# High and low halves on alternating rows of a head, moved straight from the staged tile; the second batch's norm at the start

## The chip, the cores and the metric

The kernel runs on one core of one Trainium2 chip. The core has TensorE (PE, with its weight loads shown as PEld), VectorE (DVE), ScalarE (ACT), GpSimd (POOL) and SyncE (SP), each with its own instruction stream that is carried out in order, a memory SBUF of 128 partitions, here also called rows, in which tiles live, and PSUM banks that the matmuls write. DMA transfers are issued by SP, ACT or POOL and carried out by 16 DMA engines. The metric is the time of one execution on the device in microseconds.

## The reference

Two layers, each of self-attention, cross-attention over a context, and a gated feed-forward, all with a norm before and a residual after. Four batches of 512 rows with 320 features, 20 heads of 16, a context of 1601 rows of 192. Everything is float32.

```python
def _attn(x, ctx, wq, wk, wv, wo, bo, heads):
    ...
    q = (x @ wq).reshape(b, n, heads, dh).transpose(0, 2, 1, 3)
    k = (ctx @ wk).reshape(b, j, heads, dh).transpose(0, 2, 1, 3)
    v = (ctx @ wv).reshape(b, j, heads, dh).transpose(0, 2, 1, 3)
    sim = jnp.einsum('bhid,bhjd->bhij', q, k) * scale
    a = jax.nn.softmax(sim, axis=-1)
    out = jnp.einsum('bhij,bhjd->bhid', a, v)
    out = out.transpose(0, 2, 1, 3).reshape(b, n, heads * dh)
    return out @ wo + bo
h1 = _ln(x, n1_g, n1_b)
x = _attn(h1, h1, q1, k1, v1, o1_w, o1_b, heads) + x
h2 = _ln(x, n2_g, n2_b)
x = _attn(h2, context, q2, k2, v2, o2_w, o2_b, heads) + x
h3 = _ln(x, n3_g, n3_b)
proj = h3 @ ff_w1 + ff_b1
a, g = jnp.split(proj, 2, axis=-1)
ff = a * jax.nn.gelu(g, approximate=False) @ ff_w2 + ff_b2
```

## The kernel before

**Units.** The work is cut into units: a layer, a kind (self, cross, ff), a batch and, for attention, a group of 4 heads. A layer has 20 self units (4 batches x 5 groups), then 20 cross units, then 4 feed-forward units. An attention unit goes over its keys in chunks of 128: a self unit has 4 chunks, a cross unit 13. In a chunk, `main` computes transposed scores for each of 4 heads (`st`, L1190), ScalarE takes the exponential (`pr`, L1200), and TensorE multiplies with the values (`av`, L1214); GpSimd adds the results of the chunks (L1231).

**The maximum of each row** is needed before the exponentials. It is found one or two units ahead: scores the other way round (`sps`, L990), the maximum by VectorE (L1007), at the end of which `max_end` turns the 16 columns of maxima, and four small transfers of 4 KB spread them into the rows of `nrows` (L1070). A third matmul of each score, over `nrows` and a tile of ones, subtracts the maximum. TensorE cannot start a unit's scores to their end before `nrows` has landed.

**High and low halves.** A float32 number is split into a high part (float32r) and the low rest, by GpSimd's `split` (L684, L685) into two staged tiles, `high` and `low`, whose rows are (head, feature): 64 rows for a group. In the tiles that the matmuls read, `kT` and `q`, a head has 32 rows, 16 high and then 16 low; `q` holds two such variants, high over low and low over high, so that two matmuls over 32 rows sum all four products. Since 16 rows of a head do not follow on each other in the same way in the staged tile and in `kT`, the halves go by way of memory: `move` first writes them to `kway` and `qway` (`on_way`), in a shape with heads outermost, and later reads them back into `kT` and `q` (`read_queries`, `reads`). Unit 0 alone does it with 24 transfers of 16 rows (L798), spread over the queues of SP, ACT and POOL.

**Order of the work.** The program is written out by a planner in Python. Tasks lie in chains, each with a cost and a due time in rounds; a chunk has two rounds. `steps` takes the most urgent task that is ready and for which there is credit. `both` is the projection of queries and keys of a self unit (L765), `queries` (L820) and `keys_of_context` (L849) those of a cross unit. Moves are not tasks: each unit holds a queue of them (`u.moves`), and `carry`, called at the end of `steps`, so once a chunk, emits them in the order of units, when enough rounds have passed since the unit's last one and while its `room` of 3 lasts; after them it emits `errands`, among which are the row maxima of cross units, if any room is left. All of these are issued by SP (L729 for the moves). A unit's maxima may begin four rounds after its last move was emitted (`at_hand`). `way_free` keeps a third unit from being projected while two are on the way; `free` and `unread` keep reads out of buffers whose former reader has scores left to emit.

**The start** is written by hand at the end of the function: batch 0 is loaded and normed, unit 0 projected, moved at once, its maxima found between projections for unit 1, and so on. `load_x(1)` is issued after the maxima of unit 0; the second batch's norm runs later as tasks.

**The output** of a batch goes to memory (`oway`, L1105) and comes back as `aT` with rows (head, feature) (L1114), beside `wo` in the same row order, for the output projection (L1124).

## Time and profile before

| | us |
|---|---|
| median of 3 runs | 3357.38 (3355.6 to 3358.45) |
| the profiled execution | 3351.58 |
| its span, first to last instruction | 3349.8 |

The profile is of one execution; its time is the one beside it in the table, and durations from it are compared with that one. Shares of busy time are means over stages of quite different kind. Some lines of the page beside those that are shown with the argument:

```profile
DVE  4667877776776777622237878776766767775221
ACT  2556667676676676821126765677767767776110
...
DMA packets 208849, 243.49 MB, mean 73 GB/s; under 512 B 60440, under 2 KB 140452, under 8 KB 208484
## 3 DMA queue, kind: packets, MB, share of 16 engines
q1 hardware_dynamic: 207900, 237.76, 22.7%
...
HBM read 129.25 MB, written 106.89 MB: 70 GB/s over the span
```

The two rows of digits are the busy tenths of VectorE and ScalarE in 40 equal slices of the span: the two low places, in the middle and at the end, are the feed-forward stages. The queue q1 is that of SP and carries nearly all that is moved.

### The profile page before, as it was taken

How to read it: one execution, taken by the hardware profiler on the slowest of the kernel's cores; microseconds unless marked ns; L12 is line 12 of the kernel's file. 1: busy time of each engine (PE TensorE's matmuls, PEld its weight loads, DVE VectorE, ACT ScalarE, POOL GpSimd, SP SyncE). 2: the span in 40 equal slices, each digit the busy share in tenths (PEclk: the TensorE clock that was granted, in tenths of full speed). 3: DMA queues.
4: the chain of work that ended last, by engine and by line, in shares of the span. 5: the costliest groups of instructions: out<-in, count | busy, mean ns of one | idle time of the engine just before them, and what ended most of it. 6: DMA issues, size and time to landing. Idle time of an engine off the chain costs nothing.

```text
span 3349.8 us, 81113 instructions
## 1 busy us (share of the span) xinstructions
PE 3113.5 (93%) x34290; PEld 1642.0 (49%) x34290; DVE 2105.4 (63%) x2841; ACT 1965.0 (59%) x3909; POOL 1131.7 (34%) x1230
## 2 busy tenths in 40 slices
PE   7889999899898899999999999998989989999999
PEld 4445445455444445445554554544544544543555
DVE  4667877776776777622237878776766767775221
ACT  2556667676676676821126765677767767776110
POOL 2334233434433433400213432344344344333000
PEclk7899999899998999999999999999998999999999
DMA  3344223212212222110014332322212212212000
GB/s 92 109 135 142 92 91 91 88 59 69 89 63 66 79 75 62 57 40 0 28 52 129 126 121 76 103 67 70 75 54 76 76 53 76 75 42 74 9 10 15
DMA packets 208849, 243.49 MB, mean 73 GB/s; under 512 B 60440, under 2 KB 140452, under 8 KB 208484
## 3 DMA queue, kind: packets, MB, share of 16 engines
q1 hardware_dynamic: 207900, 237.76, 22.7%
q8 instruction: 269, 4.41, 0.5%
q14 instruction: 96, 0.79, 0.1%
q0 software_dynamic: 288, 0.27, 0.0%
q10 hardware_dynamic: 296, 0.27, 0.0%
HBM read 129.25 MB, written 106.89 MB: 70 GB/s over the span
## 4 chain that ended last, share of the span: by engine, by line
PE 69%; DMA 11%; DVE 9%; ACT 5%; SPq 4%; issue 2%; POOL 1%; ACTq 0%; POOLq 0%; DVEq 0%
PE st L1190 20%; PE av L1214 16%; PE fps L1320 8%; PE yps L1374 5%; DVE pm L1007 4%; DMA nrows<-turned 4%; ACT pr L1200 3%; DMA q<-qway 3%; PE sps L990 3%; PE vps L932 3%; PE kps L849 3%; PE ops L1124 2%; PE qkps L765 2%; PE fps L1333 2%; SPq L1070 2%
## 5 line engine op out<-in xcount | busy, mean ns | idle before, releaser
L1200 ACT ACTIVATE pr<-st 128x512 f32<-128x512 f32 (+1 forms) x2720 | 1405.2, 603 | 511.6 <-PE st L1190 447.8
L1007 DVE TENSOR_REDUCE pm<-sps 128x2 f32<-128x1024 f32 (+1 forms) x987 | 1134.7, 1188 | 288.6 <-PE sps L990 175.5
L1231 POOL TENSOR_TENSOR o<-o,vo 128x512 f32<-128x512 f32 x576 | 739.7, 1284 | 1442.5 <-ACT vo L1230 1406.4
L1190 PE MATMUL st<-q,kT 32*128 32x512 f32 (+1 forms) x5120 | 980.2, 452 | 23.5 <-DVE pm L1007 7.2
L990 PE MATMUL sps<-kT,q 32*128 32x512 f32 x4800 | 874.2, 454 | 67.2 <-DMA q<-qway 37.9
L1214 PE MATMUL av<-pr,vals 128*32 128x512 f32 (+1 forms) x5440 | 774.6, 638 | 37.9 <-ACT pr L1200 31.9
L1190 PEld LDWEIGHTS st<-q,kT 32*128 32x128 f32 (+1 forms) x5120 | 478.9, 187 | 527.9 <-ACT pr L1200 301.9
L1190 PE MATMUL st<-nrows,ones 32*128 32x512 f32 (+1 forms) x2720 | 645.9, 414 | 92.8 <-DMA nrows<-turned 92.6
L1007 DVE TENSOR_REDUCE nmax<-sps 128x2 f32<-128x1024 f32 (+1 forms) x349 | 380.1, 1129 | 178.1 <-PE sps L990 146.9
L990 PEld LDWEIGHTS sps<-kT,q 32*128 32x128 f32 x4800 | 389.6, 193 | 122.6 <-DVE pm L1007 33.4
L1190 PEld LDWEIGHTS st<-nrows,ones 32*128 32x128 f32 (+1 forms) x2720 | 334.0, 189 | 138.6 <-DMA nrows<-turned 103.9
L1230 ACT COPY vo<-av 128x512 f32<-128x512 f32 x576 | 347.8, 604 | 71.9 <-PE av L1214 65.8
L1320 PE MATMUL fps<-hT,w 128*128 128x512 f32 x640 | 284.3, 597 | 0.2 <-DVE hid L1344 0.2
L1343 ACT ACTIVATE gl<-fps,b 128x512 f32<-128x512 f32 x80 | 50.7, 684 | 372.3 <-PE fps L1333 271.9
L1214 PEld LDWEIGHTS av<-pr,vals 128*32 128x32 f32 (+1 forms) x5440 | 112.8, 110 | 312.8 <-ACT pr L1200 300.0
L1344 DVE SCALAR_TENSOR_TENSOR hid<-fps,b,gl 128x512 f32<-128x512 f32 x80 | 56.4, 747 | 260.6 <-ACT gl L1343 260.6
L1320 PEld LDWEIGHTS fps<-hT,w 128*128 128x128 f32 x640 | 119.1, 190 | 148.8 <-issue 143.8
L1374 PE MATMUL yps<-w,hid 128*128 128x320 f32 x640 | 175.7, 434 | 0.4 <-ACT hT L529 0.4
L1374 PEld LDWEIGHTS yps<-w,hid 128*128 128x128 f32 x640 | 120.5, 190 | 55.8 <-issue 6.6
L1124 PEld LDWEIGHTS ops<-wo,aT 112*32 112x32 f32 (+1 forms) x3072 | 97.7, 111 | 63.3 <-issue 29.2
L1124 PE MATMUL ops<-wo,aT 112*32 112x160 f32 (+1 forms) x3072 | 125.9, 302 | 0.9 <-DVE pm L1007 0.5
L765 PE MATMUL qkps<-hT,wqk 112*128 112x256 f32 (+1 forms) x480 | 125.0, 405 | 0.9 <-DVE hid L1344 0.9
(92 smaller groups left out, 2424.2 us busy)
## 6 DMA issues: line engine op xcount, KB each, us to landing
kway<-stages SPq DMA_DIRECT2D x160, 224.0 KB
q<-qway SPq DMA_DIRECT2D x138, 256.0 KB
kT<-kway SPq DMA_DIRECT2D x80, 384.0 KB
oway<-o SPq DMA_DIRECT2D x80, 256.0 KB
qway<-high SPq DMA_DIRECT2D x160, 64.0 KB
qway<-high SPq DMA_DIRECT2D x78, 128.0 KB
kT<-kway SPq DMA_DIRECT2D x39, 256.0 KB
aT<-oway SPq DMA_DIRECT2D x32, 224.0 KB
```

The lines of the kernel that those rows point to most:

```text
L765: nc.tensor.matmul(ps[:, :w], lhsT=wqk[:n, k, u.g].rearrange("p i d -> p (i d)"), rhs=first.hT[:n, k, at : at + w], start=(k == 0), stop=( ...
L849: nc.tensor.matmul(ps[i * GD : (i + 1) * GD, :w], lhsT=wk_q[rows, k, u.g * GD : (u.g + 1) * GD], rhs=first.kvT[rows, k, i * HALF : i * HAL ...
L990: nc.tensor.matmul(ps, lhsT=u.q[j * SLOT : (j + 1) * SLOT, e, t * P : (t + 1) * P], rhs=u.kT[j * SLOT : (j + 1) * SLOT, u.k0 + s * 512 : u ...
L1007: nc.vector.tensor_reduce(to[:, j : j + n], part, AX.X, ALU.max, negate=(ns == 1))
L1124: nc.tensor.matmul(ps[f : f + m, : D // 2], lhsT=aT[:n, k, t * P + f : t * P + f + m], rhs=wo[:n, k, cols], start=(k == 0), stop=(k == 2),)
L1190: nc.tensor.matmul(st[:r, :], lhsT=ones[rows, :r] if e == 2 else u.keys(rows, c), rhs=u.rows[rows, :] if e == 2 else u.q[rows, e, :], star ...
L1200: nc.scalar.activation(p[:r], st[:r], AF.Exp)
L1214: nc.tensor.matmul(ps[j * SLOT : (j + 1) * SLOT, :], lhsT=columns_of[:r, head : head + SLOT], rhs=pr.pop((c, j))[:r, :], start=True, stop= ...
L1230: nc.scalar.copy(vo, ps)
L1231: nc.gpsimd.tensor_tensor(u.o, u.o, vo, ALU.add)
L1320: nc.tensor.matmul(ps, lhsT=w1[:, k, i * FF + c * P : i * FF + (c + 1) * P], rhs=u.hT[:, k, :], start=ahead and k == 0, stop=not ahead and ...
L1374: nc.tensor.matmul(ps[:, :D], lhsT=hid[c][:, t * P : (t + 1) * P], rhs=w2[:, c, :], start=(c == 0), stop=(c == NHC - 1),)
```

## The change

In `kT` and `q` the rows of a head now alternate: row 2d of its 32 is the high part of feature d, row 2d + 1 the low one (in the second variant of `q` the other way round). So the 64 staged rows of one half go to every second of the 128 rows, and one transfer does it, from tile to tile. The tiles in memory and the reading back are gone. A self unit has 3 moves (keys, two variants of queries), each of 2 transfers of 128 KB; a cross unit has 3 moves of keys (two halves of the columns, the ends) and 4 of queries (2 halves of the columns by 2 variants), each again of 2 transfers. `carry` has a room of 4, of which each move takes 2, and a unit's first move waits for `GAP` rounds, 3, or 4 for context keys; the later ones for none. Every move waits for the target's buffer to be free before it is emitted, where before the writes to memory did not. `staging_free` takes the place of `way_free`: the unit before last must have moved its queries; `keys_free`: all moves of earlier keys must have been emitted. At the start, all units' moves alternate between the queues of SP, ACT and POOL.

`wo` and `aT` are loaded with the feature outermost in their rows and the head inside it, both in the same way.

The second batch's input is loaded right after unit 0's moves, and its statistics, roots and normalising (10 tasks) run right after the maxima of unit 0, while the start is still on, which puts the roots on VectorE and not on GpSimd.

```diff
@@ -42,6 +42,7 @@
 HALF = QT // 2
 NHC = FF // P
 AHEAD = 8
+GAP = 3
 
 PARTS = [(0, 2 * HG), (2 * HG, H)]
 
@@ -219,7 +220,12 @@
         ]
 
     def load_out(l, name):
-        return load_rows(wo, ws[l][name], DK)
+        return [
+            lambda k=k, at=at, n=n: dma(
+                out=wo[:n, k, :], in_=ws[l][name][at : at + n, :].rearrange("(j d) c -> d j c", d=DH)
+            )
+            for k, at, n in DK
+        ]
 
     def load_cross(l):
         def quarter(t, n, i):
@@ -272,7 +278,7 @@
 
             self.moves = {"k": deque(), "q": deque()}
             self.moving = {"k": 0, "q": 0}
-            self.open = 2 if self.cross else 1
+            self.open = 7 if self.cross else 3
             self.keyed = None
             self.when = None
             self.vmade = [0, 0]
@@ -583,9 +589,7 @@
     saved = [dram.tile([P, KB, QT + 32], F32, name=f"ctxT{b}") for b in range(B)]
     saved_tail = [dram.tile([CK[0][2], 2, TAIL], F32, name=f"tail{b}") for b in range(B)]
 
-    q_way = [dram.tile([HG, 3, DH, N], F32, name=f"qway{i}") for i in range(2)]
-    k_way = [dram.tile([HG, 2, DH, 2, 4 * (HALF + 32)], F32, name=f"kway{i}") for i in range(2)]
-    users = {"q": [], "k": []}
+    users = []
     o_way = [dram.tile([H, SLOT, N], F32, name=f"oway{i}") for i in range(2)]
 
     def add_context(l, b, put, due, free):
@@ -665,20 +669,17 @@
 
     def carry():
 
-        room = 3
+        room = 4
         for _, what, u in sorted(movers):
             todo = u.moves[what]
-            while todo and todo[0][1]() and clock["round"] >= u.moving[what] + 3 - todo[0][3] and room > 0:
-                room -= todo[0][2]
+            while todo and todo[0][1]() and clock["round"] >= u.moving[what] + todo[0][2] and room > 0:
+                room -= 2
                 todo.popleft()[0]()
             if not todo:
                 movers.remove((u.i, what, u))
         while errands and room > 0 and clock["round"] >= errands[0][0] and errands[0][1]():
             errands.popleft()[2]()
 
-    def by_rows(t):
-        return t.rearrange("j h d n -> j (h d) n")
-
     def split(low, high):
 
         nc.gpsimd.tensor_copy(high.bitcast(F32R), low)
@@ -716,45 +717,42 @@
                 add(chain, 0.0, hold, due - 4, yes, lambda: "h" in u.own)
 
         def staged():
+            users.append(u)
             return (two.tile([P, N], F32, tag=n, name=n) for n in ("low", "high"))
 
-        def move(of, n, pairs, may=None):
+        def move(of, pairs, may, gap=0):
 
             def f():
-                if may is None:
-                    pending[of] -= 1
+                pending[of] -= 1
                 u.moving[of] = clock["round"]
-                for i, (to, src) in enumerate(pairs()):
-                    queue = (nc.sync, nc.scalar, nc.gpsimd)[i % 3] if start["on"] and u.i == 0 else nc.sync
-                    queue.dma_start(out=to, in_=src)
-                if may is not None:
-                    u.open -= 1
-                    if not u.open:
-                        u.when = -9 if start["on"] else clock["round"]
-
-            if may is None:
-                pending[of] += 1
-            u.moves[of].append((f, may or yes, n, may is None))
+                for to, src in pairs():
+                    queue = nc.sync
+                    if start["on"]:
+                        queue = (nc.sync, nc.scalar, nc.gpsimd)[room["first"] % 3]
+                        room["first"] += 1
+                    queue.dma_start(out=to.bitcast(F32), in_=src)
+                u.open -= 1
+                if not u.open:
+                    u.when = -9 if start["on"] else clock["round"]
+
+            pending[of] += 1
+            u.moves[of].append((f, may, gap))
             u.moving[of] = clock["round"]
             if (u.i, of, u) not in movers:
                 movers.append((u.i, of, u))
 
-        def on_way(what):
-
-            users[what].append(u)
-            return (q_way if what == "q" else k_way)[len(users[what]) % 2]
-
-        def way_free(what):
-
-            return not (what == "k" and pending[what]) and (len(users[what]) < 2 or not any(users[what][-2].moves.values()))
-
-        def read_queries(t, keys=None):
-
-            def pairs():
-                reads = [(u.q[:, e].bitcast(F32), by_rows(t[:, e : e + 2])) for e in range(2)]
-                return ([(u.kT[:, u.k0 : u.k0 + N].bitcast(F32), by_rows(keys))] if keys is not None else []) + reads
-
-            move("q", 2 if keys is None else 3, pairs, lambda: unread() and (u.cross or free()))
+        def staging_free():
+            return len(users) < 2 or not users[-2].moves["q"]
+
+        def keys_free():
+            return not pending["k"]
+
+        def move_queries(high, low, cols, may, gap):
+            for e in range(2):
+                move(
+                    "q", lambda e=e: [(u.q[(e + h) % 2 :: 2, e, cols], t) for h, t in enumerate((high, low))],
+                    may, 0 if e else gap,
+                )
 
         def both(part):
 
@@ -783,29 +781,13 @@
                 return
             if u.i:
                 split(low, high)
-            if u.i == 0:
-                for j in range(HG):
-                    for t in range(2):
-                        for h in range(2):
-                            of = (high, low)[h]
-                            slot = slice(j * SLOT + h * DH, j * SLOT + (h + 1) * DH)
-                            away = slice(j * SLOT + (1 - h) * DH, j * SLOT + (2 - h) * DH)
-                            rows = slice(j * DH + t * GD, j * DH + t * GD + DH)
-                            to = [u.kT[slot, u.k0 : u.k0 + N]] if t else [u.q[slot, 0, :], u.q[away, 1, :]]
-                            for x in to:
-                                queue = (nc.sync, nc.scalar, nc.gpsimd)[room["first"] % 3]
-                                room["first"] += 1
-                                queue.dma_start(out=x.bitcast(F32), in_=of[rows, :])
-                u.when = -9
-                u.keyed = True
-                first.made["q"] += 1
-                first.made["k"] += 1
-                return
-            to_k = on_way("k").rearrange("j h d i n -> j h d (i n)")[:, :, :, :N]
-            to_q = on_way("q")
-            move("q", 2, lambda: [(to_k[:, 0], high[GD:]), (to_k[:, 1], low[GD:])])
-            move("q", 3, lambda: [(to_q[:, e], t[:GD]) for e, t in enumerate((high, low, high))])
-            read_queries(to_q, to_k)
+            def may():
+                return unread() and free()
+
+            move(
+                "q", lambda: [(u.kT[h::2, u.k0 : u.k0 + N], t[GD:]) for h, t in enumerate((high, low))], may, GAP,
+            )
+            move_queries(high[:GD], low[:GD], slice(0, N), may, 0)
             u.keyed = True
             first.made["q"] += 1
             first.made["k"] += 1
@@ -827,14 +809,9 @@
             low, high = staged()
             nc.scalar.mul(low[:, :w], ps[:, :w], DH**-0.5)
             split(low[:, :w], high[:, :w])
-            to_q = on_way("q")
             for i in range(2):
                 rows = slice(i * GD, (i + 1) * GD)
-                cols = slice(i * w, (i + 1) * w)
-                lo, hi = (t[rows, :w] for t in (low, high))
-                pairs = [(to_q[:, e, :, cols], t) for e, t in enumerate((hi, lo, hi))]
-                move("q", 3, lambda pairs=pairs: pairs)
-            read_queries(to_q)
+                move_queries(high[rows, :w], low[rows, :w], slice(i * w, (i + 1) * w), unread, 0 if i else GAP)
             u.keyed = True
             first.made["q"] += 1
 
@@ -859,20 +836,21 @@
             nc.vector.tensor_copy(low[:, 1:3, :], pair[:, :, : HALF + 32])
             split(room["low"], room["high"])
 
-            to_k = on_way("k")
-            for i in range(2):
-                rows = slice(i * GD, (i + 1) * GD)
-                pairs = [(to_k[:, h, :, i], t[rows].rearrange("p a w -> p (a w)")) for h, t in enumerate((high, low))]
-                move("k", 2, lambda pairs=pairs: pairs)
-            of = to_k.rearrange("j h d i (a w) -> (j h d) i a w", a=4)
-
-            def reads():
-                to = u.kT.bitcast(F32)
-                full = to[:, : 4 * QT].rearrange("p (a w) -> p a w", a=4)
-                pairs = [(full[:, :, i * HALF : (i + 1) * HALF], of[:, i, :, :HALF]) for i in range(2)]
-                return pairs + [(to[:, 4 * QT :].rearrange("p (a w) -> p a w", a=4), of[:, 1, :, HALF:])]
-
-            move("k", 3, reads, free)
+            parts = high, low
+
+            def full(i):
+                to = u.kT[:, : 4 * QT].rearrange("p (a w) -> p a w", a=4)
+                return [
+                    (to[h::2, :, i * HALF : (i + 1) * HALF], t[i * GD : (i + 1) * GD, :, :HALF]) for h, t in enumerate(parts)
+                ]
+
+            def ends():
+                to = u.kT[:, 4 * QT :].rearrange("p (a w) -> p a w", a=4)
+                return [(to[h::2], t[GD:, :, HALF:]) for h, t in enumerate(parts)]
+
+            move("k", lambda: full(0), free, GAP + 1)
+            move("k", lambda: full(1), free)
+            move("k", ends, free)
             first.made["kv"] += 1
 
         def unread():
@@ -883,12 +861,12 @@
 
         if not u.cross:
             for part in range(2):
-                add(chain, (0.46,) * 3, lambda part=part: both(part), due - 2 + 2 * part, lambda part=part: part or way_free("q") and way_free("k"))
+                add(chain, (0.46,) * 3, lambda part=part: both(part), due - 2 + 2 * part, lambda part=part: part or staging_free())
         else:
-            add(chain, 2.45, keys_of_context, keys_due, lambda: way_free("k"))
+            add(chain, 2.45, keys_of_context, keys_due, keys_free)
             if u.g == 0:
                 add(chain, 0.0, hold, due - 4, yes, lambda: "h" in u.own)
-            add(chain, (0.477,) * 3, queries, due - 2, lambda: way_free("q"))
+            add(chain, (0.477,) * 3, queries, due - 2, staging_free)
 
     def quarter_banks(name):
 
@@ -1111,7 +1089,7 @@
                 held["read"] += 1
                 aT = one.tile([P, 3, N], F32, tag="aT", name="aT")
                 for k, at, n in DK:
-                    dma(out=aT[:n, k, :], in_=way[at // DH : (at + n) // DH, :DH, :])
+                    dma(out=aT[:n, k, :], in_=way[at // DH : (at + n) // DH, :DH, :].rearrange("j d n -> d j n"))
                 end(aT)
 
             errands.append((clock["round"] + 4, lambda: held["open"] < 1, read))
@@ -1512,6 +1490,7 @@
     warm(5)
     until(lambda: not chains["proj"], "proj")
     at_once(units[0])
+    now(load_x(1))
     add_proj(units[1])
     add_values(units[0])
     first = units[0]
@@ -1527,7 +1506,8 @@
     run("values")
     max_reduce(first)
     max_end(first)
-    now(load_x(1))
+    for _ in range(2 * NQ + 2):
+        run("norm")
     loads.extend(load_x(2))
     for fs in (load_out(0, "o1_w"), load_x(3), load_cross(0)):
         loads.extend(fs)
```

## The prediction

> **What bounds the kernel now.** I read the page first (busy shares, chain), then the waits of TensorE, then the same waits stage by stage, then the clock, then the order of SyncE's queue around two of the waits.
>
> ```profile
> span 3349.8 us, 81113 instructions
> PE 3113.5 (93%) x34290; PEld 1642.0 (49%) x34290; DVE 2105.4 (63%) x2841; ACT 1965.0 (59%) x3909; POOL 1131.7 (34%) x1230
> ...
> PE 69%; DMA 11%; DVE 9%; ACT 5%; SPq 4%; issue 2%; POOL 1%; ACTq 0%; POOLq 0%; DVEq 0%
> ```
> ```profile
> core 0: 3349.8 us, clock 0.952
> ```
> ```profile
> PE st L1190 <- DMA nrows<-turned: 92.6, 33, 7.2
> PE sps L990 <- DMA q<-qway: 37.9, 19, 5.8
> PE av L1214 <- ACT pr L1200: 31.9, 130, 0.5
> PE sps L990 <- DVE pm L1007: 10.0, 24, 1.3
> PE sps L990 <- DMA kT<-low: 8.8, 2, 8.6
> ```
>
> TensorE is the bound: busy 93%, the others 63% and less. It idles 236 us (3349.8 - 3113.5), and three waits for DMAs hold 139.3 us of that (92.6 + 37.9 + 8.8); none of the waits for an engine comes near them in length. Beside the idle time there is clock: at 0.952 granted, 0.048 x 3349.8 = 161 us of full-speed time were withheld. Now the same by stage; the stages are start, self-attention, cross-attention and feed-forward of layer 0, then self, cross and feed-forward of layer 1.
>
> ```profile
> 0.00:130.00 130.00, 104.10 (x841) 56.99 (x841) 70.81 (x126) 50.38 (x101) 42.38 (x63) 0.84 0.35 99
> 130.00:455.00 325.00, 291.72 (x3506) 161.65 (x3511) 236.65 (x363) 194.68 (x391) 112.29 (x133) 0.94 0.35 115
> 455.00:1433.00 978.00, 901.12 (x11774) 466.34 (x11762) 695.04 (x846) 701.68 (x1412) 394.53 (x371) 0.94 0.25 75
> 1433.00:1740.00 307.00, 305.35 (x1355) 164.36 (x1348) 80.97 (x172) 48.41 (x80) 40.88 (x95) 1.00 0.07 23
> 1740.00:2095.00 355.00, 328.08 (x4010) 181.34 (x4009) 280.12 (x401) 230.99 (x464) 128.13 (x146) 0.98 0.34 112
> 2095.00:3066.00 971.00, 904.04 (x11784) 466.50 (x11788) 680.65 (x809) 703.88 (x1413) 394.15 (x371) 0.94 0.23 71
> ```
>
> The columns are the length, the busy time of PE, PEld, DVE, ACT and POOL, then granted clock, DMA share, GB/s. The feed-forward stage has no such waits and runs at clock 1.00. That the clock falls *because* of the waits is seen at one of them:
>
> ```profile
> 1270.00:1316.00 46.00, 45.07 (x657) 24.56 (x660) 35.68 (x42) 35.61 (x72) 21.79 (x18) 1.00 0.23 70
> 1316.00:1321.00 5.00, 1.31 (x16) 0.30 (x8) 2.35 (x2) 1.22 (x3) 1.26 (x1) 1.00 0.24 74
> 1321.00:1330.00 9.00, 8.73 (x88) 5.92 (x88) 2.56 (x3) 3.85 (x9) 1.26 (x1) 0.62 0.49 138
> ```
>
> Forty-six microseconds without a wait at clock 1.00 and 98% busy; then TensorE works 1.31 of 5 us, and the next 9 us get 0.62. So a wait is paid about twice. Why the small row transfers are late:
>
> ```profile
> 2287.72 5.48 SPq L729 DMA_DIRECT2D kway<-stages  x4
> 2293.30 4.64 SPq L1070 DMA_DIRECT2D nrows<-turned  x4
> ...
> 2944.78 2.73 SPq L729 DMA_DIRECT2D kway<-stages  x2
> 2947.62 3.90 SPq L1070 DMA_DIRECT2D nrows<-turned  x4
> ...
> 2743.59 2.59 SPq L1070 DMA_DIRECT2D nrows<-turned  x4
> ```
> ```profile
> L685 POOL TENSOR_TENSOR stages<-stages 128x896 f32<-128x896 f32 x40 | 84.2, 2106 | 3.2
> L684 POOL CAST stages<-stages 128x896 fp32r<-128x896 f32 x40 | 37.2, 931 | 58.0 <-DVE stages L859 45.7 <-DVE nmax L1050 11.1 <-DMA kT<-kway 1.3
> ```
>
> SyncE issues in order. A key write to memory (kway) is emitted one chunk after the keys were computed, so SyncE stands until GpSimd's split (0.93 + 2.11 us) has made the low half, and the four transfers of the row maxima (nrows) stand behind it. Then these four themselves take 3.9 to 4.6 us to issue; with nothing ahead of them they take 2.59, the last row. The queries are late for another reason, the way through memory, in the chain:
>
> ```profile
> 22.60 1.84 DMA kT<-low
> ...
> 1154.55 5.23 DMA qway<-high
> 1159.79 9.69 DMA q<-qway
> ```
>
> Out 5.23 us, back 9.69: 14.9 us, of 64 KB and 256 KB transfers, where a direct 32 KB one from staged rows to keys landed in 1.84.
>
> **The change part by part.** *1, the direct moves.* A self unit issues 8 transfers now (2 of keys and 3 of queries at 128 KB, 3 reads at 256 KB, 1408 KB in all) and then 6 of 128 KB (768 KB). A cross unit issues 15 (4 x 224, 2 x 384, 64, 6 x 64, 2 x 256 KB, 2624 KB) and then 14 (4 x 192, 2 x 32, 8 x 64 KB, 1344 KB). Over 40 units of each kind 161,280 KB become 84,480, and 920 issues become 800. What is left on the path per unit is one landing in place of two. The trace has no 128 KB copy between rows of SBUF: from below it costs the 1.84 us of the 32 KB one, from above the 9.69 us of the longest read of 256 KB. I take about 2.5, nearest the direct copy, since the read goes to memory first and is twice as large.
>
> The Trainium skill (DMA: Bandwidth & Descriptors, "Why a DMA increments its semaphore by 16 and not by 1") says that a transfer is spread over as many engines, up to 16, as divide the slowest dimension of both its sides. By it the way out and back, laid out by four heads, would run on 4 engines, and a copy of 64 rows on 16; that agrees with 5.23 and 9.69 against 1.84, and by its 16 engines the 2.5 would rather be too much.
>
> The times of emission move too. `carry` is called once a chunk, that is every 2 rounds. Cross keys went out at 2 and 4 rounds and were read at 8; now two moves go at 4 and the ends at 6. Queries: 2, 4 and 8 become 4 and 6. So GpSimd has a chunk more before SyncE meets its semaphore, and everything is handed over a chunk sooner. Where keys are computed at chunk 10 of 13 (the second collision above, by the place of their matmuls among the exponentials), nrows is now emitted at chunk 11, ahead of the keys. Where they are computed at chunk 9 (the first collision), the two moves use up the room of 4, nrows goes to the next `carry`, behind six key transfers; SyncE reaches it some 3 us after the split ends, about where it does now, but the transfers behind which it lands are a third of the bytes. I leave 1 to 3 us there.
>
> Added waits: a move now waits for the target buffer itself, with SyncE's queue behind it (nrows, context, output, weights), but `may` emits it only after the last score of the buffer's former reader was emitted, so SyncE waits for a chunk at most. The staged tile is held until its move has landed; ScalarE's next write into it could stand, with the exponentials behind it. Bound: nothing, up to 2 us in each of 80 units. I take nothing, as two tiles alternate and the unit before last must have moved already.
>
> *2, the start.* The 24 transfers of unit 0 become 6. The first scores waited 8.6 us for the last of them; GpSimd, which issues a third, is still behind its bias additions, so I take 2 us off. Units 1 and 2 no longer go through memory: 7 of the 8.1 us below. The second batch's norm adds DVE work there:
>
> ```profile
> L509 DVE TENSOR_SCALAR hn<-x,mv,root 128x320 f32<-128x320 f32 (+1 forms) x128 | 67.0, 570 | 15.7 <-POOL root L473 15.4
> L493 DVE BATCH_NORM_STATS2 st<-x 128x6 f32<-128x320 f32 x96 | 44.9, 468 | 2.1 <-DMA x<-in_x_dram 2.1
> ```
>
> 4 x 0.57 + 4 x 0.47 and about 20 tiny root and aggregate operations, an estimate of 7 us by these two rows; it is moved, not added, and DVE has 59 idle us of the 130. If its cover is gone it costs up to 3 us where the maxima queue behind it. In exchange batch 1's queries come sooner: between 0 and 10 us, I take 5.
>
> *3, output weights and read in another row order.* Same counts and bytes, no wait of TensorE named them: nothing, either way.
>
> **The sum**, with the waits of each stage:
>
> ```profile
> PE sps L990 <- DMA kT<-low: 8.8, 2, 8.6
> PE sps L990 <- DMA q<-qway: 8.1, 2, 5.8
> ...
> PE st L1190 <- DMA nrows<-turned: 8.8, 5, 4.0
> PE sps L990 <- DMA q<-qway: 6.5, 5, 2.7
> ...
> PE st L1190 <- DMA nrows<-turned: 38.8, 13, 7.2
> PE sps L990 <- DMA q<-qway: 14.4, 7, 2.6
> ...
> PE st L1190 <- DMA nrows<-turned: 7.8, 5, 4.6
> ...
> PE st L1190 <- DMA nrows<-turned: 37.3, 10, 6.5
> PE sps L990 <- DMA q<-qway: 8.9, 5, 2.2
> ```
>
> The withheld clock is (1 - clock) x length: 20.8, 19.5, 58.7, 7.1 and 58.3 us. I choose shares: 85% of the waits and 75% of the clock in the cross stages, less in self-attention, whose first chunks also wait for DVE.
> - start: 9 of waits, 6 of clock (after the first scores TensorE is still cold): 15
> - self, layer 0: 0.8 x 15.3 + 0.7 x 19.5 = 26
> - cross, layer 0: 0.85 x 53.2 + 0.75 x 58.7 = 89
> - self, layer 1: 0.8 x 7.8 + 0.5 x 7.1 = 10
> - cross, layer 1: 0.85 x 46.2 + 0.75 x 58.3 = 83
> - batch 1 sooner: 5
>
> Sum 228 us. The profiled execution took 3351.6 us, 1.8 above its span and 5.8 below the median of the runs, 3357.4. So 3351.6 - 228 + 5.8 = 3129, said as **3130**. All of the waits and 0.9 of the clock would be 139 + 148 = 287: 3070.
>
> **The rivals.**
> - *The row maxima stay late* (keys' moves take the room, nrows stays behind them). Then 0.85 x 76.1 us of cross waits and, by their share of the waits (three quarters), 66 us of clock stay: the gain falls by 131 to 97, 3260. For it: the chunk-9 pattern. Against: the other pattern, and 4 us issues that come with 4 x 224 KB on few engines.
> - *The clock does not come back.* Its loss has other causes than these waits, and they stay. Of the 228, 117 are clock (6 + 14 + 44 + 4 + 44, and 5 for batch 1); without them 3357 - 111 = 3246. Against it stands 1316 to 1330 above, where the clock fell right behind one wait. The Trainium skill (TensorE: Matmul & The Clock Gate, "Part 1: The HAM clock gate") speaks for it: the clock is halved after a window of some 3.4 us without work, so that by it the many shorter waits would cost no clock.
> - *The halves wait for each other.* If the two interleaved halves of a pair count as overlapping, the second waits for the first to land, 1.84 us or more, seven times a cross unit: 13 us of SyncE standing, queries little sooner, nrows behind three such pairs. I give it half of the second rival's gain: 3300. This is also the case that the change does not do what it says.
> - *Slower: SyncE stands at a taken buffer.* A move that waits for scores not yet run, a chunk in every unit (978 us / 260 chunks = 3.8 us), would hold nrows past its slack; in each of 38 cross units that is 3.8 us of wait and as much of clock, 289 us, against 76 + 88 now; and ScalarE held 2 us in 40 self units adds 80. With the other gains (97): 3357 + 289 - 164 + 80 - 97 = 3465. It decides from a standing of about 3 us, an estimate: nrows have some two chunks, 7.6 us, less 2.6 us for their issue and about 2 for landing. Against it: `free` and `unread` in the emission.
>
> **How the numbers follow.** Forecast 0.64, late maxima 0.14, clock stays 0.07, halves wait 0.07, slower 0.05, and 0.03 near no change. The range goes from 3070 (everything gone) to 3262, which takes in the late maxima and the clock, and leaves out 0.15 and the forecast's own edges. What a measurement of this kernel can tell from no change is about 0.2%, 7 us. Faster 0.92, within 0.03, slower 0.05.
>
> **What would show it.** Right: q1 near 160 MB (237.76 now), waits of TensorE for nrows under 20 us and for queries under 8, clock at 0.98 to 0.99, a cross stage of 880 to 900 us. Part 1 wrong in nrows: that wait row still above 60 us, with key moves before it in SyncE's rows. Wrong in the clock: waits gone and clock still 0.95. Wrong in the pairs: gaps of 2 us between two issues of one move. Wrong at the start: first exponentials no sooner than now, with DVE norm rows before the maxima. Wrong as a whole if a wait for DVE or ScalarE takes their place in TensorE's waits.

## The result, and the profile after

| | before | after |
|---|---|---|
| median of the runs | 3356.49 us (4 runs, 3346.51 to 3358.45) | 3116.77 us (4 runs, 3111.1 to 3121.78) |
| the profiled execution | 3351.58 us | 3113.44 us |
| its span | 3349.8 us | 3111.7 us |

The changed kernel takes 0.9291 of the time, with a 95% interval of 0.9265 to 0.9317: 239.7 us less by the medians. The forecast was 3130, in a range of 3070 to 3262. Two executions were disturbed and stand in no time, ratio or trace here (the 3135.9 that one expectation names still counts the first): the profiled one of the first run with eight row transfers (clock 0.844; that kernel's trace comes from a second run), and one of the kernel before beside that run (12,675 us).

From the page of the changed kernel: the span, the engines' busy time, the granted clock in 40 slices, the queue q1 (packets, MB, share of 16 engines) and the shares of the chain that ended last.

```profile
span 3111.7 us, 81138 instructions
...
PE 2997.5 (96%) x34290; PEld 1601.3 (51%) x34290; DVE 2115.3 (68%) x2834; ACT 1961.0 (63%) x3909; POOL 1129.4 (36%) x1213
...
PEclk8999999999999999999999999999999999999999
...
q1 hardware_dynamic: 187240, 159.28, 20.1%
...
HBM read 43.53 MB, written 28.90 MB: 23 GB/s over the span
...
PE 78%; DVE 14%; ACT 5%; issue 1%; POOL 1%; SPq 0%; DMA 0%; ACTq 0%; POOLq 0%; DVEq 0%
```

TensorE idled 236.3 us before and 114.2 now (3111.7 - 2997.5): 122 us. Its busy time fell from 3113.5 to 2997.5 with the same 34290 matmuls: 116 us, which I put down to the clock: the withheld clock, (1 - clock) x span, fell from 161 to 22 us, and some of that lay in time in which TensorE idled. Both add up to the 238 us of the span. Transfers held 11% of the chain that ended last, SyncE's queue 4%; now both hold 0%.

The waits of TensorE after: us in total, times, longest.

```profile
PE av L1192 <- ACT pr L1178: 25.5, 119, 0.6
PE sps L968 <- DVE pm L985: 19.5, 40, 1.1
PE sps L968 <- DVE nmax L985: 12.6, 16, 3.8
PE st L1168 <- DVE pm L985: 8.8, 15, 0.8
PE st L1168 <- DVE x L1109: 8.2, 19, 0.9
PE sps L968 <- DMA q<-high: 7.0, 1, 7.0
```

One wait for a transfer is left, that of the first scores of all. The rows of maxima (92.6 us in 33 waits) and the way through memory (37.9 in 19) are gone. What leads now are short waits for ScalarE and VectorE, 0.2 to 0.8 us on the mean; VectorE's maxima for `sps` went from 10.0 to 19.5 us, a small part of the gain given back.

The same stages as in the prediction, cut at about the same points of the program, told by the first and last exponentials of each stage (columns as there: length, busy PE, PEld, DVE, ACT, POOL, granted clock, DMA share, GB/s):

```profile
0.00:115.00 115.00, 95.69 (x839) 56.36 (x840) 75.86 (x143) 51.16 (x102) 41.55 (x56) 0.90 0.38 94
115.00:403.00 288.00, 269.77 (x3446) 152.81 (x3445) 233.43 (x349) 192.76 (x387) 109.53 (x124) 0.99 0.34 87
403.00:1296.00 893.00, 866.40 (x11818) 452.34 (x11815) 698.34 (x842) 700.66 (x1413) 395.11 (x371) 0.99 0.22 55
1296.00:1600.00 304.00, 301.45 (x1242) 161.74 (x1242) 80.06 (x172) 47.33 (x76) 40.99 (x95) 1.00 0.05 14
1600.00:1943.00 343.00, 323.76 (x4080) 182.73 (x4078) 278.05 (x400) 231.44 (x466) 127.95 (x146) 1.00 0.32 81
1943.00:2828.00 885.00, 861.19 (x11831) 450.39 (x11834) 688.39 (x803) 702.61 (x1414) 394.93 (x371) 1.00 0.20 50
2828.00:3111.00 283.00, 279.21 (x1044) 144.93 (x1044) 61.17 (x127) 35.01 (x54) 19.37 (x51) 1.00 0.04 13
```

| stage | forecast gain | measured (length before - after) |
|---|---|---|
| start | 15 | 15 |
| self, layer 0, with batch 1 sooner | 26 + 5 | 37 |
| cross, layer 0 | 89 | 85 |
| feed-forward, layer 0 | 0 | 3 |
| self, layer 1 | 10 | 12 |
| cross, layer 1 | 83 | 86 |

Why the transfers were late can be seen in one place of the kernel before, and of the kernel after, by the DMA share (the mean of 16 engines) and the rate. Before, TensorE waits for queries in it:

```profile
1164.00:1168.00 4.00, 1.24 (x24) 0.84 (x18) 1.23 (x2) 1.93 (x4) 1.35 (x2) 1.00 0.28 102
```

After, six transfers of keys, one of context and the next of queries run:

```profile
1026.00:1032.00 6.00, 6.00 (x64) 2.40 (x56) 5.40 (x6) 5.67 (x13) 3.16 (x3) 1.00 0.93 237
```

Before, TensorE works 1.24 of 4 us while only 0.28 of the 16 engines move anything: little over four engines, and the rest stand idle. After, 0.93 of them work. Counted over the whole trace, in slices of 0.5 us by packets under way, the kernel before had 892 us with 3.6 to 4.6 packets at once, the kernel after 49 us. The semaphore events give each transfer's time from issue to landing (median, and longest in brackets), and how many separate updates it made:

| transfer | before | updates | after | updates |
|---|---|---|---|---|
| row maxima, 4 KB | 4.3 us (9.8) | 9 | 1.7 us (3.4) | 9 |
| self queries, 128 KB, first hop / direct | 9.8 (12.2) | 5 | 2.4 (4.9) | 16 |
| queries, 256 KB, second hop | 7.4 (11.9) | 5 | none | |
| cross keys, 224 KB first hop / 192 KB direct | 7.0 (13.3) | 5 | 3.5 (5.3) | 16 |
| cross keys, 384 KB, second hop | 4.3 (11.1) | 16 | none | |

The Trainium skill (DMA: Bandwidth & Descriptors, "Why a DMA increments its semaphore by 16 and not by 1") says that the sequencer writes the share of the unused engines at once, and each engine used adds one. By that rule five updates are four engines and one for the rest, and sixteen are sixteen engines; the plateau at four packets agrees. By its rule too, a transfer takes the lowest-numbered engines, so that the maxima's, with nine updates on eight engines, would share all four of them; no trace here numbers the engines. By these counts the transfers with four heads outermost ran on four engines, whatever their size, and the small ones of the maxima landed 2.6 us later than they now do.

### The profile page after: what moved, and what is told of

Same layout as the page of the kernel before. It is cut to its first block, busy times and chain, and to the rows that moved or that the text cites. A ratio compares the mean times of both kernels' runs of the same rounds, so it can differ in the third digit from the quotient of the medians.

```text
span 3111.7 us, 81138 instructions
## 1 busy us (share of the span) xinstructions
PE 2997.5 (96%) x34290; PEld 1601.3 (51%) x34290; DVE 2115.3 (68%) x2834; ACT 1961.0 (63%) x3909; POOL 1129.4 (36%) x1213
## 3 DMA queue, kind: packets, MB, share of 16 engines
q1 hardware_dynamic: 187240, 159.28, 20.1%
## 4 chain that ended last, share of the span: by engine, by line
PE 78%; DVE 14%; ACT 5%; issue 1%; POOL 1%; SPq 0%; DMA 0%; ACTq 0%; POOLq 0%; DVEq 0%
PE st L1168 23%; PE av L1192 18%; PE fps L1298 9%; DVE pm L985 6%; PE yps L1352 6%; PE qkps L763 4%; ACT pr L1178 4%; PE kps L826 3%; PE sps L968 3%; PE vps L910 3%; PE ops L1102 3%; PE fps L1311 2%; DVE nmax L985 2%; PE qps L802 2%; PE vps L892 2%
## 5 line engine op out<-in xcount | busy, mean ns | idle before, releaser
L1168 PE MATMUL st<-q,kT 32*128 32x512 f32 (+1 forms) x5120 | 951.5, 436 | 19.8 <-DVE x L1109 8.2
L968 PE MATMUL sps<-kT,q 32*128 32x512 f32 x4800 | 840.2, 437 | 39.3 <-DVE pm L985 19.5
L1192 PE MATMUL av<-pr,vals 128*32 128x512 f32 (+1 forms) x5440 | 736.8, 608 | 32.3 <-ACT pr L1178 25.5
L1168 PEld LDWEIGHTS st<-q,kT 32*128 32x128 f32 (+1 forms) x5120 | 468.2, 180 | 495.3 <-ACT pr L1178 277.1
L1168 PE MATMUL st<-nrows,ones 32*128 32x512 f32 (+1 forms) x2720 | 631.1, 395 | 0.1
L968 PEld LDWEIGHTS sps<-kT,q 32*128 32x128 f32 x4800 | 363.9, 183 | 91.5 <-DVE pm L985 52.4
```

Source lines behind the costliest of these rows:

```text
L968: nc.tensor.matmul(ps, lhsT=u.q[j * SLOT : (j + 1) * SLOT, e, t * P : (t + 1) * P], rhs=u.kT[j * SLOT : (j + 1) * SLOT, u.k0 + s * 512 : u ...
L1168: nc.tensor.matmul(st[:r, :], lhsT=ones[rows, :r] if e == 2 else u.keys(rows, c), rhs=u.rows[rows, :] if e == 2 else u.q[rows, e, :], star ...
L1192: nc.tensor.matmul(ps[j * SLOT : (j + 1) * SLOT, :], lhsT=columns_of[:r, head : head + SLOT], rhs=pr.pop((c, j))[:r, :], start=True, stop= ...
```

## The experiments

All times are medians; each ratio is against the kernel before, run beside it on the same chip. Between these sets the kernel before itself had medians of 3352.1 to 3356.5, so that a few microseconds between rows of different sets mean little; early keys and norm later are of one set, old row order, two queues and norm in the gap of another.

| | us | ratio, 95% | idle PE, us | clock | waits for nrows, us |
|---|---|---|---|---|---|
| before | 3356.5 | 1 | 236.3 | 0.952 | 92.6 |
| before, later key writes | 3271.3 | 0.9755 (0.9735 to 0.9774) | 189.2 | 0.966 | 31.4 |
| before, wide on the way | 3157.9 | 0.9417 (0.9399 to 0.9435) | 118.9 | 0.984 | 13.4 |
| before, wide and later | 3158.2 | 0.9414 (0.9396 to 0.9432) | 117.4 | 0.987 | 2.0 |
| after | 3116.8 | 0.9291 (0.9265 to 0.9317) | 114.2 | 0.993 | 0 |
| after, early keys | 3115.3 | 0.9293 (0.9278 to 0.9308) | 114.0 | 0.992 | 0 |
| after, norm later | 3123.7 | 0.9318 (0.9302 to 0.9334) | 114.9 | 0.992 | 0.3 |
| after, old row order of wo and aT | 3120.0 | 0.9305 (0.9289 to 0.9321) | 113.1 | 0.991 | 0 |
| after, two queues at the start | 3116.8 | 0.9292 (0.9277 to 0.9308) | 112.0 | 0.992 | 0 |
| after, norm in VectorE's gap | 3107.9 | 0.9268 (0.925 to 0.9287) | 109.2 | 0.994 | 0 |
| the last, early keys too | 3110.5 | 0.9271 (0.9257 to 0.9284) | 108.3 | 0.992 | 0 |
| after, eight row transfers | 3134.9 | 0.9343 (0.9328 to 0.9358) | 130.3 | 0.991 | 8.8 |

For the eight row transfers time and ratio are of the first run, the other columns of the second. Idle PE is the span less the busy time of that kernel's profile. In the expectations, theory A is that the small transfers were late because the large ones ran on few engines; theory B, that SyncE stood before its split, and that the halves took two hops.

### Wide on the way

The kernel before, still by way of memory, with the same transfers, bytes and times of emission; only the rows alternate (in unit 0's 24 transfers too), so that every transfer on the way has 64 or 128 rows outermost and not 4 heads.

```diff
-    q_way = [dram.tile([HG, 3, DH, N], F32, name=f"qway{i}") for i in range(2)]
-    k_way = [dram.tile([HG, 2, DH, 2, 4 * (HALF + 32)], F32, name=f"kway{i}") for i in range(2)]
+    q_way = [dram.tile([GD, 3, N], F32, name=f"qway{i}") for i in range(2)]
+    k_way = [dram.tile([GD, 2, 2, 4 * (HALF + 32)], F32, name=f"kway{i}") for i in range(2)]
...
-                pairs = [(to_q[:, e, :, cols], t) for e, t in enumerate((hi, lo, hi))]
+                pairs = [(to_q[:, e, cols], t) for e, t in enumerate((hi, lo, hi))]
...
-                pairs = [(to_k[:, h, :, i], t[rows].rearrange("p a w -> p (a w)")) for h, t in enumerate((high, low))]
+                pairs = [(to_k[:, h, i], t[rows].rearrange("p a w -> p (a w)")) for h, t in enumerate((high, low))]
...
```

> The kernel before, still by way of memory and with its times of emission, issues and bytes, but with the new alternating rows, so that each write and read of qway and each write of kway has 64 or 128 rows outermost and not 4 heads. Theory A (the way was slow because its transfers ran on few DMA engines, and these engines then held up the row maxima): queries land in 3 to 5 us and not 7 to 9, nrows in about 2, TensorE's wait for nrows falls from 92.6 to under 45 us, and with its clock the time is 3160 to 3230. Theory B (what cost was SyncE standing at GpSimd's split and the second hop itself): the waits for nrows stay over 65 us and the time is 3290 to 3350.

It took 3157.9: 195 us less than the kernel before beside it (3353.4), and a little better than A's range. q1 moved 237.80 MB, as before. The second hop of the queries landed after 3.7 us in place of 7.4, the first hop of the cross keys after 3.0 in place of 7.0, the row maxima after 1.7 in place of 4.3. The waits of TensorE for transfers in it:

```profile
PE st L1190 <- DMA nrows<-turned: 13.4, 9, 2.0
PE sps L990 <- DMA kT<-low: 7.9, 1, 7.9
```

No wait for queries is left, though they still go out and come back. And this is what the maxima that still wait wait for, in SyncE's queue of the same kernel (start, us, instruction):

```profile
2285.16 2.69 SPq L729 DMA_DIRECT2D kway<-stages  x2
2287.95 2.65 SPq L1070 DMA_DIRECT2D nrows<-turned  x4
```

SyncE stands at a key write as it did before, but the four rows behind it take 2.65 us to issue, where the prediction's rows show 3.90 and 4.64. Over the whole trace, the 23 sets of four that the kernel before issued within 9 us of a key write took 4.16 us in the median, and its 15 others 2.59; in the wide run they took 2.65 (21 sets) and 2.68 (17). And SyncE stood no less at GpSimd's split of the keys. Its waits for the start of that split, in the kernel before, in this run and in the changed kernel (us in total, times, longest):

```profile
SPq L729 <- POOL stages L684: 383.9, 36, 19.1
...
SPq L729 <- POOL stages L684: 432.8, 40, 23.5
...
SPq L733 <- POOL stages L685: 33.9, 5, 8.5
```

The slices with about four packets at once fell from 892 to 53 us, with 4% more packets for the same bytes. So most of the gain, 195 of some 240 us, is the shape of the transfers and not the hop that was left out. A holds.

### Later key writes

The kernel before with the first key write two rounds later, so that SyncE no longer meets GpSimd's split with the maxima behind it; the shapes stay narrow.

```diff
-            while todo and todo[0][1]() and clock["round"] >= u.moving[what] + 3 - todo[0][3] and room > 0:
+            while todo and todo[0][1]() and clock["round"] >= u.moving[what] + 3 - todo[0][3] + 2 * (what == "k" and len(todo) == 3) and room > 0:
```

> The kernel before with one thing changed: the first write of a cross unit's keys goes out 4 rounds after the keys and not 2, so that SyncE does not meet an unfinished split. Theory B (SyncE standing): waits for nrows fall by half or more, 3230 to 3290. Theory A (load on few engines): the collisions only move to other units, nrows waits stay over 70 us, 3320 to 3370.

3271.3, in B's range. The waits of TensorE in it:

```profile
PE sps L990 <- DMA q<-qway: 45.6, 22, 6.0
PE st L1190 <- DMA nrows<-turned: 31.4, 14, 4.9
```

The maxima's waits fell to a third, the queries' stayed: standing in the queue was a real part of the maxima's lateness. In half-microsecond slices 905 us still had about four packets at once.

### Wide and later

Both edits at once, to see whether the standing is what is left between 3158 and 3117.

> The kernel before, still by way of memory but with alternating rows (64 or 128 rows outermost on that way), which took 3158, and in it the first key write at 4 rounds in place of 2. What is left between it and the changed kernel is 41 us. Theory 'standing': SyncE still meets GpSimd's split at the key write with nrows behind it (13.4 us of nrows waits and their clock); with later keys these go and the time is 3130 to 3145. Rival 'the way through memory itself and the start': the maxima's waits are small already, so the time stays at 3150 to 3162, and later keys may make kT the wait.

3158.2 (3149.3 to 3161.0), against 3157.9 without the later writes: the rival's range. The waits for nrows did go, from 13.4 to 2.0 us, and the profiled execution was 8 us shorter than that of the run before (3147.1 against 3155.5), but the median didn't follow. The order of the queue was worth 82 us while the transfers were narrow (3353.4 less 3271.3), and nothing measurable once they were wide.

### Early keys

The changed kernel with its first cross key move at 2 rounds in place of 4, to see whether its later emission, which the forecast counted on, does anything.

```diff
-            move("k", lambda: full(0), free, GAP + 1)
+            move("k", lambda: full(0), free, 2)
```

> The changed kernel with the keys' first move 2 rounds after the keys, as the first write was before, and not 4. Theory B: SyncE stands at the split again with nrows behind it, in about half of the 38 cross units for 2 to 4 us with as much of clock again: 3190 to 3260, nrows waits 40 to 90 us. Theory A: the transfers are quick now and nrows lands in 2 us, so waits for nrows stay under 15 us: 3110 to 3145.

3115.3, no wait for nrows at all, the same as the changed kernel. But the run tests less than it was meant to. In the changed kernel none of the 38 sets of maxima in the cross stages has a key move within 9 us ahead of it, and in this run none has either (23 had one in the kernel before, 21 in the wide run). By the code, a move also waits until its target's buffer is free (`free`), and in most units that comes later than the rounds: the first key move goes out 2.4 to 15 us behind the keys' matmuls in both, where the first write to memory went out after 2.3 to 3.3. So SyncE stood at the split in 10 units (60.5 us) in place of 5, never with the maxima behind it. What standing costs with wide transfers is told by the run before this one.

### The norm of batch 1

Three runs. First, the changed kernel with the load and norm of batch 1 back where they were.

```diff
-    now(load_x(1))
...
-    for _ in range(2 * NQ + 2):
-        run("norm")
+    now(load_x(1))
```

> The changed kernel with the second batch's load and norm where they were before. If the early norm is worth what was forecast (5 us, between 0 and 10): 3117 to 3127, and unit 4 or 5 waits longer for its queries. A rival: the norm on DVE at the start costs as much as it brings (TensorE waits 3.8 us for a maximum just behind it), then within 3 us of 3117.

3123.7 (3121.2 to 3126.0): the early norm is worth about 7 us, or 8 against the early keys of the same set (3114.3 to 3116.4). But it has a price at the start. VectorE in the changed kernel, from the last steps of the root on, and TensorE's wait then:

```profile
43.17 1.51 DVE L515 TENSOR_SCALAR hn<-x,mv,root 128x320 f32<-128x320 f32 x4
44.60 2.35 DVE L985 TENSOR_REDUCE nmax<-sps 128x2 f32<-128x1024 f32 x2
...
45.87 1.23 PE L968 MATMUL sps<-kT,q 32*128 32x512 f32 x8 [3.80 <-DVE nmax L985]
```

The maxima of unit 1 queue behind the norm, 36.3 to 44.7 us, and TensorE waits 3.80 us; a stretch of 6.8 us at half clock follows. Between 17.3 and 24.7 us the same VectorE has nothing to do. So the second run uses that gap, with batch 1 loaded ahead and the first moves on two queues.

```diff
-                        queue = (nc.sync, nc.scalar, nc.gpsimd)[room["first"] % 3]
+                        queue = (nc.sync, nc.scalar)[room["first"] % 2]
...
     load_bias(0, 1)
+    now(load_x(1))
...
     at_once(units[0])
-    now(load_x(1))
+    for _ in range(2 * NQ + 2):
+        run("norm")
...
     max_end(first)
-    for _ in range(2 * NQ + 2):
-        run("norm")
```

> As the run with two queues at the start, and batch 1 loaded before batch 0's norm, with its norm run as soon as unit 0's moves are issued, where VectorE is idle from 17 to 25 us in the changed kernel, and not behind the maxima of unit 0. Theory 'the early norm's price is the wait of 3.8 us for the maxima at 46 us, and the low clock of 6.8 us behind it': both go, 3105 to 3113. Rival 'DVE's place doesn't matter, the gain of the early norm is all in unit 4': 3113 to 3118, and if the norm pushes the evictions of the next projections back, up to 3122.

3107.9 (3104.1 to 3114.1). In its trace the norm ends where the first maxima begin, and those begin 0.1 us later than in the changed kernel (24.78 against 24.67 us):

```profile
23.35 1.51 DVE L515 TENSOR_SCALAR hn<-x,mv,root 128x320 f32<-128x320 f32 x4
24.78 3.77 DVE L985 TENSOR_REDUCE nmax<-sps 128x2 f32<-128x1024 f32 x4
```

The wait of 3.80 us and the low clock behind it are gone; in the first 115 us the clock is at half for 17.1 us in place of 23.9. The median is 9 us, or 0.3%, under the changed kernel's. The third run is the two queues alone.

> The changed kernel with the moves of the start on the queues of SP and ACT alone. In the changed kernel the two moves on GpSimd's queue are issued at 19.3 and 20.1 us, behind its addition of the bias to x (16.1 to 19.4 us), and the first scores wait 7.0 us. Theory 'GpSimd's queue is what the first scores wait for': that wait falls to 4 to 5.5 us, first scores at 21 to 22 us in place of 23.3, time 1 to 4 us under the changed kernel's 3117. Rival 'the landing of 128 KB and the split before it, not the queue': the wait stays at 6.5 to 7.5 us and the time within 2 us.

3116.8 (3114.8 to 3118.1). The first scores' wait fell from 7.0 to 4.5 us and 0.9 more, so GpSimd's queue was part of it (its addition to x runs from 16.06 to 19.36 us and its two moves go out behind it). The time is the changed kernel's, and its fastest execution is slower than the slowest with the norm in the gap, which was run beside it. The gain of about 9 us is therefore that of the norm's place, with the earlier load that it needs, and not of the queues.

### Early keys and the norm in the gap

> The changed kernel with both edits that were quicker or as quick alone: the norm of batch 1 in VectorE's gap at the start with two queues (3107.9) and the first key move at 2 rounds (3115.3 against 3116.8). Theory 'the gains are apart': 3104 to 3110, no nrows waits. Rival 'an earlier key move shifts the schedule's other waits': 3110 to 3120.

3110.5 (3109.0 to 3111.4), where the two ranges meet, just inside the rival's: nothing beyond the norm in the gap alone.

### The old row order of the output weights

```diff
-                    dma(out=aT[:n, k, :], in_=way[at // DH : (at + n) // DH, :DH, :].rearrange("j d n -> d j n"))
+                    dma(out=aT[:n, k, :], in_=way[at // DH : (at + n) // DH, :DH, :])
```

and `load_out` with rows in their old order.

> The changed kernel with the output weights and the attention output read back in the old row order (head outermost). The forecast put part 3 of the change at nothing. Theory 'nothing': no wait of TensorE named aT or wo before or after, so the time stays within 4 us of the changed kernel's 3117 and no wait for a DMA of aT appears. Rival 'few engines again': the read with 4 or 8 heads outermost runs on few engines, lands later (5 us in place of 3.3), and holds up the small transfers of the maxima and queries that are issued about it: nrows waits of 5 to 20 us come back, 3125 to 3150, clock at or under 0.985.

3120.0 (3117.6 to 3124.1): at most 3 us over the changed kernel, and the two ranges overlap. aT's transfers make 7 or 8 updates in place of 16 and land after 4.5 to 5.4 us in place of 3.3 to 3.4, and nothing of TensorE waits for them. This part of the change shows no gain that the runs can tell.

### What a wait costs

The changed kernel with the row maxima's four transfers issued as eight of half the size, to bring short waits back with nothing else changed.

```diff
-                queue.dma_start(out=slots[:, :, part], in_=turned[part, :])
+                if u.cross and u.before.cross:
+                    for e in range(2):
+                        half = slice(i * SLOT + e * DH, i * SLOT + (e + 1) * DH)
+                        queue.dma_start(out=slots[e * DH // NQ : (e + 1) * DH // NQ, :, part], in_=turned[half, :])
+                else:
+                    queue.dma_start(out=slots[:, :, part], in_=turned[part, :])
```

> The changed kernel with each of the four row transfers of a cross unit's maxima issued as two of half the size (8 issues of some 0.66 us in place of 4), nothing else. In the changed kernel the first scores of a cross unit end 4.5 us after the maxima are turned and the rows land 3.7 us after it: 0.8 us are left in most units. Four more issues take 2.0 to 2.65 us, so that waits of 1.2 to 1.9 us come back in some 27 of 38 units and shorter ones in the others: 35 to 55 us of nrows waits. Theory 'a wait is paid about twice, short ones too': the clock falls to 0.97 to 0.98 and the time is 3180 to 3230. Rival 'the clock's loss had other causes, waits under 3 us cost no clock': the clock stays at 0.99 and the time is 3150 to 3172. If the slack is larger than read here, no waits come and the time stays at 3117.

3134.9, 18 us above the changed kernel: below both ranges. The same kernel again, for its trace:

> The same kernel as the last with eight row transfers, for its trace. It took 3135.9, 19 us above the changed kernel and less than both theories said, so fewer or shorter waits came than read from the 0.8 us of slack. Theory 'a wait is paid about twice, short ones too': some 8 to 12 us of nrows waits and the clock down from 0.993 to 0.988 to 0.990. Rival 'waits under 3 us cost no clock': 16 to 20 us of nrows waits at a clock of 0.992 to 0.993.

3138.6. Its waits, and its clock:

```profile
PE st L1173 <- DMA nrows<-turned: 8.8, 17, 0.8
...
PE st L1173 <- issue: 5.6, 10, 1.2
```
```profile
core 0: 3136.5 us, clock 0.991
```

The slack had been read rightly, the delay had not. Transfers of half the size land 0.57 us after each other and not 0.66, and the first scores need only the first seven of the eight: in the unit whose maxima are turned at 503.7 us in the changed kernel and at 501.9 here, the rows that they need land 5.14 us after it, where they landed at 3.73, and the scores that stood at 4.52 us stand at 5.23. So the waits were of 0.5 to 0.8 us. The kernel idles 16 us more than the changed one (130.3 against 114.2) and its span is 25 us longer; the withheld clock went from about 22 to about 28 us. The 8.8 us of nrows waits are what the first theory said, and the clock (0.991, and 0.990 in the second execution) lies just above its 0.988 to 0.990, and at the edge of it. Yet its "short ones too" isn't borne out: the clock's part came from a few of the waits. All the lone waits of TensorE behind the first 80 us, in the traces of twelve kernels (no other wait of 0.4 us or more within 8 us, clock full when they begin), by length:

| length of the wait, us | waits | followed by half clock | us at half clock, mean over all |
|---|---|---|---|
| 0.2 to 1.0 | 819 | 16 | 0.1 |
| 1.0 to 1.4 | 25 | 7 | 1.1 |
| 1.4 to 2.0 | 10 | 6 | 2.4 |
| 2.0 to 3.0 | 19 | 15 | 4.0 |
| over 3.0 | 9 | 9 | 6.8 |

Half clock comes in pieces of 3.41 us, and half of each is lost. A wait below 1 us costs itself; one of 2 to 3 us costs itself and some 2 us more. Of the sixteen falls in the first row, eleven began in or just behind the narrow matmuls that are told of under "What stays open", so that the wait may have no part in them.

## Why the prediction was right, point by point

- **The bound and the sum.** It said that TensorE is the bound, that three waits for transfers are worth about 111 us, and the clock behind them 112 (with 5 more for batch 1). Measured were 122 us of idle time and 116 of clock, in the same stages to within 4 us, but for self-attention of layer 0, which gained 37 where 31 were said. Within a stage it is less exact, and some of the fit is errors that cancel: cross-attention of layer 0 gained 50 us of idle time and 35 of busy time, where 45 of waits and 44 of clock were said.
- **The landing.** It took about 2.5 us for a 128 KB copy between rows, from the nearer of two ends far apart; 2.4 was measured. So close a hit is in part luck, as its rows allowed anything from 1.84 to 9.69. By the rule of the Trainium skill that it named (DMA: Bandwidth & Descriptors, "Why a DMA increments its semaphore by 16 and not by 1") it would rather have been quicker; the wide run agrees with the rule in that the engines carry most of the gain.
- **Maxima and queries.** It said under 20 us of waits for nrows, under 8 for queries, 160 MB in q1, a cross stage of 880 to 900 us and a clock of 0.98 to 0.99. Measured: none, 7.0, 159.28, 893 and 885, and 0.993.
- **"I leave 1 to 3 us there", at keys of chunk 9.** This step failed, without harm. The moves of keys went out after the maxima in all 38 sets, held back by the wait for the target's buffer, to which the prediction gave no such effect; SyncE's rows of the changed kernel at the unit in which the wide run stood:

```profile
2265.02 2.60 SPq L1048 DMA_DIRECT2D nrows<-turned  x4
2267.74 0.67 SPq L733 DMA_DIRECT2D kT<-stages  x1
```

- **The slack of the maxima, "some two chunks, 7.6 us", and with it the point from which standing decides.** This was sized too large. From the turned maxima to the first scores that need them are 4.5 us in 15 of the 38 cross units that follow another, 4.8 to 5.1 in 8 more and 5.9 and over in 15, and 3.73 to 3.80 are used in most: 0.8 us of slack in the tightest, where the prediction had about 3. A standing of 1.4 us costs time already, as the eight row transfers show. Had the moves stood, the slower rival would have come sooner than it said.
- **The start.** 15 forecast, 15 measured; the first exponential begins at 41.6 us in place of 54.4. The first scores' wait fell by 1.6 us (8.6 to 7.0), where 2 were said, for the reason given: GpSimd's queue. The early norm cost 3.80 us of waiting and 6.8 us at half clock, a little more than the "up to 3" allowed; in all it was worth about 7 us, where 5 were said.
- **The rivals.** Late maxima: no wait for nrows is left. Clock doesn't come back: it did, to 0.993. The Trainium skill's rule of an idle window of about 3.4 us (TensorE: Matmul & The Clock Gate, "Part 1: The HAM clock gate") fits the pieces of 3.41 us in which the clock falls, and the waits over 3 us, all of which were followed by them; but 15 of 19 waits of 2 to 3 us were too, so a window need not be wholly idle, and the prediction's reading of the row at 1316 us was the better guide. Halves wait for each other: the issues of a pair follow on each other at once. SyncE's rows in the changed kernel, with no gap near 2 us between the two halves of a move:

```profile
1025.98 3.31 SPq L733 DMA_DIRECT2D kT<-stages  x4
1029.35 0.61 SPq L613 DMA_DIRECT2D ctxT<-ctxT  x1
1030.05 1.43 SPq L733 DMA_DIRECT2D kT<-stages  x2
1031.58 0.56 SPq L733 DMA_DIRECT2D q<-high  x1
1032.24 0.54 SPq L733 DMA_DIRECT2D q<-low  x1
```

  Slower through standing: SyncE's longest waits are now for the maxima themselves (turned, 967.0 us in 78), which it meets early and not late:

```profile
SPq L1048 <- DVE turned L1041: 967.0, 78, 57.5
```

- **Where it gave the credit.** It named two causes of the maxima's lateness side by side, SyncE's standing and slow issues. The runs put them in an order: with wide transfers the standing is worth nothing that the median shows, with narrow ones 82 us. And its sum for the direct moves goes by one landing in place of two and by fewer bytes. The wide run keeps both landings and all the bytes and has 195 of the 240 us, so that what was paid for was mostly the few engines, which the prediction had in the sentence on the rule and in a rival's "on few engines".
- **What stays open.** Between the wide run and the changed kernel are 41 us. About 7 are the early norm. In cross-attention of layer 0 the two are alike: 894 and 893 us by the cuts above, 890 and 886 from the stage's first exponential to its last. So there the hop through memory cost at most 4 us, of the 85 gained. By the same cuts 14 us lie in self-attention of layer 0, the norm's among them, 23 in cross-attention of layer 1, and the rest in between. The wide run's profile has 5 us more idle time than the changed kernel's and 39 more of busy time at the same matmuls. In its list of clock changes some 20 us at half clock follow waits for nrows, and 31 us, in three places, follow no wait over 0.4 us; at the longest of them TensorE was busy 3.31 of the 3.5 us before, and then ran at 0.51 for 17.5 us (same columns as above):

```profile
2827.00:2830.50 3.50, 3.31 (x48) 2.44 (x44) 1.43 (x2) 3.14 (x7) 1.29 (x1) 1.00 0.00 0
2830.50:2848.00 17.50, 16.80 (x91) 4.59 (x89) 2.67 (x10) 9.74 (x20) 5.08 (x4) 0.51 0.21 33
```

  All three falls begin in or just behind the scores of a unit's last keys, 32 matmuls of 66 columns where the others have 512; here are the last 15 of them, at the longest fall:

```profile
2829.62 1.07 PE L1018 MATMUL sps<-kT,q 32*128 32x66 f32 x15 [0.19 <-ACT pr L1200]
```

  Each cross unit has such a stretch. In the twelve traces, where it began at full clock, the clock fell in it or within 3.4 us behind it 3 times of 418 where it took under 2.1 us, 9 of 28 where it took 3 to 4 us, and 19 of 20 where it took longer (these hold short waits too). So a TensorE that the trace shows as busy can lose the clock as well. Whether the narrow matmuls bring it down, and what the hop costs in layer 1, these runs don't tell.

## What to carry to other kernels

A low DMA share while an engine waits for a transfer is not spare capacity: look whether the share stands at a plateau such as 4 of 16 engines, and if so give the transfer a shape with many rows outermost before leaving a hop out or reordering a queue. Small transfers on a critical path pay for the narrow ones ahead of them, and once those are wide, the order of the queue may no longer matter. At a busy TensorE, waits of some 1.4 us and more are the ones to remove first, since they cost clock besides; many of half a microsecond cost only themselves.

## What the hardware showed that was not expected

- Transfers over few engines go with a late landing of others that are much smaller: the 4 KB transfers landed after 4.3 us (median) beside narrow ones and after 1.7 beside wide ones of the same bytes, and four issues behind a key write took 4.16 us (median) against 2.65.
- A 256 KB read from memory, same bytes, took 7.4 us with four heads outermost and 3.7 with 128 rows.
- The clock can fall to half after waits much shorter than the pieces of 3.41 us in which it is granted: 7 of 25 lone waits of 1.0 to 1.4 us, 6 of 10 of 1.4 to 2.0. In the wide run it also stayed there for 17.1 us with no wait over 0.3 us ahead of it, behind matmuls of 66 columns; such stretches of over 4 us were followed by half clock in 19 of 20 cases, those under 2.1 us in 3 of 418.
